# A fused attention and edge-filter kernel: engine orders written by hand, and steps and loads placed anew

## The chip, the cores and the metric

The kernel runs on one core of a Trainium2 chip. The metric is the device time of one execution in microseconds, and the median of several runs is compared. One execution of the kernel before was also taken by the hardware profiler. In what follows PE is TensorE, PEld its weight loads, DVE VectorE, ACT ScalarE, POOL GpSimd and SP the engine whose queue issues the DMAs.

## The reference

Two layers follow each other on `x` of shape (4, 512, 64, 64), all in float32.

```python
# layer 0: linear attention with an extra convolved head set
q, k, v = h @ wq.T, h @ wk.T, h @ wv.T                  # 512 -> 512 each, per pixel
qkv = concat([q, k, v]);  dw = depthwise_5x5(qkv);  pw = grouped_1x1(dw, groups of 8)
f = concat([qkv, pw]).reshape(B, 128 heads, 3 * 8, N)
query, key, value = relu(f[:, :, :8]), relu(f[:, :, 8:16]), f[:, :, 16:]
scores = einsum('bhdn,bhen->bhde', [value; 1], key)
out = einsum('bhde,bhen->bhdn', scores, query);  out = out[:8] / (out[8] + eps)
y = conv1x1(out, proj) * inv + shift + x                # folded batch norm, residual
# layer 1: edge maps, branches, attention, fuse
sobel, lap, diag, grad = fixed 3x3 depthwise filters of y, with abs, squares and square roots
ef = gelu(batch_norm(1x1 branch of each map))           # 4 branches, 512 -> 128 each
att = sigmoid(w2 @ gelu(w1 @ mean(ef)))                 # per image
z = w_fuse @ (ef * att);  out = gelu(layer_norm(z)) + y
```

## The kernel before, in words

The work is split by image `b` (4), and in each image by group `g` of 128 channels (`NG` = 4), so there are 16 groups. An image's 4096 pixels are cut into 8 strips of 512 (`NJ`), each strip made of every fourth row of one half of the image.

**A group** runs two lists of steps. `keys_and_values` projects the keys and the values of the 8 strips (`project`, `values`), transposes the keys (`turn`) and sums scores (`scores`). Between these steps it places what is left over from the group before: correlations of the second half of the image, both query convolutions, and divisions. `queries` projects the queries, convolves the keys (`convolve(KEY, 0)` and `convolve(KEY, 1)`), transposes the result (`conv_turn`), correlates it with the values (`correlate`) and divides. `convolve` issues 160 small 32x32 matmuls, each seen twice in the trace, so 320 matmul records and 320 weight loads for each of the 64 convolutions. The two convolutions of keys are called K0 and K1 here, those of queries Q0 and Q1.

**Value patches.** `values` writes the values to a scratch in DRAM (`near<-vt`), and `load_near` reads patches of it back (`near<-near`, 1056 KB each, 8 for each group). Three are loaded at the end of `keys_and_values`; each second `correlate` step frees a buffer and loads the next. In `queries` the first, second, third and fourth such load come after `co(0, 0)`, `co(0, 2)`, `co(1, 0)` and `co(1, 2)`; the last three of these stand directly ahead of K1, with no projection among them.

**Behind the groups** of image b + 1 runs what remains of image b, as three generators: `project_out` (Y: 32 steps, `yps` matmuls, `y` stored to DRAM), `edge_branches` (E: for 16 windows and 2 channel pairs the edge maps on DVE and ACT, then `br` matmuls) and `fuse_out` (F: `zps` matmuls, layer norm, output). Each generator yields a share of time, and `advance` runs its next step when the foreground's steps have used up as much (`pace`). The last image has no groups behind which it could run: its Y, E and F, and the F of image 2, are the tail. In the tail half of Y runs alone, then one step of the rest (second half of Y, then F of image 2) follows each yield of E, then F of image 3 runs alone.

**Order.** `tc.manual_schedule(engines={PE})` (L98) keeps the PE's instructions in the order in which the code issues them. The instructions of DVE, ACT and POOL, and the DMAs of the SP queue, are put in order by the scheduler, from its own costs. Each engine then runs its list strictly from the front, and a DMA whose data is not ready holds up those behind it. `ps` tiles in PSUM have 4 buffers, and the `quad` tiles 4.

Of the kernel before, what the change touches and what calls it, by code (L numbers as in the profile page):

```python
# [65 lines left out]

WAIT_Y, WAIT_E, WAIT_F = 20.0, 12.0, 16.0
# [13 lines left out]
def conv_seq_kernel(  # L81
# [16 lines left out]
    ctx.enter_context(tc.manual_schedule(engines={mybir.EngineType.PE}))  # L98
# [72 lines left out]

    def load_constants():
        nc.sync.dma_start(out=consts_sb, in_=consts)
        nc.sync.dma_start(out=vec_sb, in_=vec)
        nc.sync.dma_start(out=batt1_sb, in_=batt1)

        nc.scalar.activation(inv0, vec_sb[:, V_BNV, :], AF.Sqrt, bias=bn0_eps)
        nc.vector.reciprocal(inv0, inv0)
# [3 lines left out]

        gamma_row = work_tile("gamma_row")
        nc.sync.dma_start(out=inv0_row, in_=bn0[1])
        nc.sync.dma_start(out=gamma_row, in_=bn0[0])
        nc.scalar.activation(inv0_row, inv0_row, AF.Sqrt, bias=bn0_eps)
# [25 lines left out]

    xs = {}

    class Group:
# [15 lines left out]
        def load_mat(self, t):  # L231

            dp = gw.tile([P, 4, 48], F32, name="dp_sb", tag="dp_sb", bufs=2)
            nc.sync.dma_start(out=dp, in_=dpk[self.g, t // QUERY])
            self.mat[t] = gw.tile([P, 4, 40, 8], F32, name="mat", tag="mat")
            nc.gpsimd.tensor_tensor(  # L236
                self.mat[t],
                dp[:, :, 0:40].unsqueeze(3).to_broadcast([P, 4, 40, 8]),
                dp[:, :, 40:48].unsqueeze(2).to_broadcast([P, 4, 40, 8]),
                ALU.mult,  # L240
            )

        def load_x(self, j):
            xs[self.b, j] = []
            for n in range(2):
                xt = xst.tile([P, 2, 512], F32, name="xt")
                nc.sync.dma_start(out=xt, in_=x[self.b, j, :, 2 * n : 2 * n + 2, :])
                xs[self.b, j] += [xt[:, 0, :], xt[:, 1, :]]

        def project(self, t, j):  # L250
            half, k = STRIPS[j]
            if (self.b, j) not in xs:
                self.load_x(j)
# [5 lines left out]
            if t == QUERY and not (j in KV_ORDER[:2] and self.g < NG - 1):  # L259
                del xs[self.b, j]  # L260
# [4 lines left out]
            for n in range(4):  # L265
                nc.sync.dma_start(out=inps[t][r::4, n, b : b + 8, :], in_=rows(s)[32 * n : 32 * n + 32, :, :])
# [6 lines left out]
        def values(self, j):  # L273
# [8 lines left out]
            if j not in Q_ORDER[:2]:  # L282
                del xs[self.b, j]
# [5 lines left out]
            for a in range(2):  # L289
                for jp in range(2):  # L290
                    nc.sync.dma_start(
                        out=self.near_dram[jp, b + a : b + a + 7 : 2, 2 : W + 2, (k + 2) % 4, :].rearrange(
                            "c x d -> x c d"
                        ),
                        in_=vt[64 * a : 64 * a + 64, :, 2 * jp : 2 * jp + 2, :].rearrange("p c q d -> p c (q d)"),
# [37 lines left out]
        def fold_turn(self):  # L333
# [4 lines left out]
            nc.scalar.copy(self.st, t_ps[:, 0:P])  # L338
            self.p = work_tile("p")
            nc.sync.dma_start(out=self.p, in_=proj[self.g])  # L340

        def fold(self):
# [4 lines left out]
            nc.sync.dma_start(out=self.folded[0, :, self.g, :], in_=f)  # L347
# [24 lines left out]
        def divide(self, half):  # L372
            banks = self.spread_out(self.rec)
            for k in range(4):
# [3 lines left out]
                nc.sync.dma_start(out=self.heads[j, :, self.g, :], in_=q)  # L378
# [90 lines left out]
        def mix(self):  # L469

            self.pc = work_tile("pc")
            if self.b:
                nc.sync.dma_start(out=self.pc, in_=mixed[self.g])
                return
            rest = work_tile("projc")
            nc.sync.dma_start(out=rest, in_=projc[self.g])
            pw = mini.tile([P, 8], F32, name="pw")
            nc.sync.dma_start(out=pw, in_=pwk[self.g])
            pwb = mini.tile([P, 16, 8], F32, name="pwb", bufs=1)
            nc.vector.tensor_mul(  # L480
                pwb, bdmask.rearrange("p (h d) -> p h d", d=8), pw.unsqueeze(1).to_broadcast([P, 16, 8])
            )
            ps = ps_tile("mix")
            nc.tensor.matmul(ps, lhsT=pwb.rearrange("p h d -> p (h d)"), rhs=rest, start=True, stop=True)
            nc.scalar.copy(self.pc, ps)
            nc.sync.dma_start(out=mixed[self.g], in_=self.pc)
# [32 lines left out]
        def conv_fold(self):  # L519
# [5 lines left out]
            nc.sync.dma_start(out=self.folded[1, :, self.g, :], in_=f)  # L525
# [9 lines left out]
        def conv_divide(self, half):  # L535
            banks = self.spread_out(self.crec)
            for i in range(4):
                q = work_tile("cq")
                nc.vector.tensor_mul(q, self.conv[QUERY][i], banks[i])
                nc.sync.dma_start(out=self.cheads[half, self.g, i], in_=q)  # L540
# [3 lines left out]
        def keys_and_values(self, before):  # L544
# [12 lines left out]
            def q(method, *args):  # L557
                t = {"convolve": T_CONV, "correlate": T_CORR}.get(method, T_SMALL)
                return [(t, lambda: getattr(before, method)(*args))] if before else []

            def co(jp, first):
                return q("correlate", 1, jp, first) + q("correlate", 1, jp, first + 1)

            return sum([
                pj(KEY, 0), q("conv_sums"), pj(VALUE, 0), q("divide", 0), pj(KEY, 1), pj(VALUE, 1), co(0, 0), tr(0),
                pj(KEY, 2), co(0, 2), pj(VALUE, 2), sc(0), tr(1), co(1, 0), pj(KEY, 3), co(1, 2), pj(VALUE, 3), sc(1), tr(2),
                q("convolve", QUERY, 0), pj(KEY, 4), q("mix"), q("conv_weights"), sc(2), tr(3), pj(VALUE, 4),
                q("conv_heads"), q("conv_denominators", 0), pj(KEY, 5), q("conv_fold"), q("conv_divide", 0), sc(3), tr(4),
                pj(VALUE, 5), q("convolve", QUERY, 1), pj(KEY, 6), sc(4), tr(5), q("conv_denominators", 1), pj(VALUE, 6),
                [(0.0, self.load_wtab)], pj(KEY, 7), q("conv_divide", 1), sc(5), tr(6), pj(VALUE, 7),  # L570
                [(0.0, lambda: self.load_near(VALS))],
            ], [])

        def queries(self):
# [14 lines left out]
            def own(method, *args):  # L589
                return [(T_SMALL, lambda: getattr(self, method)(*args))]  # L590

            return sum([
                pj(0), own("scores", KV_ORDER[6]), own("turn", KV_ORDER[7]), pj(1), cv(0), pj(2), own("scores", KV_ORDER[7]), ct(0, 0), ct(0, 1), pj(3),
# [434 lines left out]
```

## Time and profile before

| | us |
|---|---|
| median of 3 runs (5157.64 to 5178.55) | 5158.51 |
| the profiled execution | 5156.95 |
| its span, first to last instruction | 5155.2 |
| PE busy in the span | 4721.2 |
| DVE busy | 2125.2 |
| ACT busy | 1622.7 |
| POOL busy | 384.0 |

The mean granted PE clock is 0.963 of full speed. The time of the profiled execution and its span differ by 1.75 us, which lie outside the first and last instruction. The groups fill the span up to about 4437 us; the tail is what follows.

### The profile page before, as it was taken

Reading aid. Unit: us, or ns where it says so; the run is one execution under the profiler, and the core shown is the slowest. Engines: PE = TensorE matmul, PEld = TensorE weight load, DVE = VectorE, ACT = ScalarE, POOL = GpSimd, SP = SyncE. Lnnn points to the kernel's source line nnn. Section 1 sums busy time; section 2 is a strip of 40 time slices with the busy share of each in tenths; the row PEclk is TensorE's granted clock in tenths of the full one; section 3 lists DMA queues with packets and bytes.
Section 4 is the critical chain, followed back from the end, with each engine's and each line's share of the span. In section 5 each row is a group of like instructions: output and inputs, shape, how many; then the busy total and the mean of one; then the engine's idle time right before and its main releaser. Section 6 shows DMA issues by size and latency. Waiting matters only on the chain. (4 is left out here: it accounts for less than half of the span.)

```text
span 5155.2 us, 107053 instructions
## 1 busy us (share of the span) xinstructions
PE 4721.2 (92%) x46362; PEld 2727.4 (53%) x46362; DVE 2125.2 (41%) x2960; ACT 1622.7 (31%) x2585; POOL 384.0 (7%) x291
## 2 busy tenths in 40 slices
PE   7899999998999999799999998989989998899877
PEld 4556555454566655344466655444446565345443
DVE  1222221113655625211456543431135556246975
ACT  1111111001444524200235442430024445125765
POOL 0000000000000003200000000320000000000225
PEclk9999999999999999899999999999999999899989
DMA  6777777775666666767667666567666665674535
GB/s 184 187 193 195 185 212 191 179 160 140 194 184 193 194 191 188 212 153 150 168 178 208 170 191 186 180 202 172 154 177 173 178 183 160 176 179 117 153 103 169
DMA packets 645992, 910.30 MB, mean 177 GB/s; under 512 B 323688, under 2 KB 394376, under 8 KB 627088
## 3 DMA queue, kind: packets, MB, share of 16 engines
q1 hardware_dynamic: 645520, 903.45, 65.5%
q8 instruction: 364, 5.96, 0.5%
q14 instruction: 108, 0.88, 0.1%
HBM read 622.13 MB, written 213.98 MB: 162 GB/s over the span
## 5 line engine op out<-in xcount | busy, mean ns | idle before, releaser
L256 PE MATMUL proj<-xt,w_sb 128*128 128x512 f32 x2048 | 959.6, 611 | 58.3 <-DMA xt<-in_x 47.2
L642 PE MATMUL yps<-hd,fold_sb 128*128 128x512 f32 x2048 | 904.3, 598 | 25.2 <-DMA hd<-heads 23.1
L390 PE MATMUL cv<-inp,mat 32*32 32x512 f32 x20480 | 771.7, 621 | 121.2 <-issue 112.0
L256 PEld LDWEIGHTS proj<-xt,w_sb 128*128 128x128 f32 x2048 | 382.8, 195 | 534.8 <-issue 457.1
L642 PEld LDWEIGHTS yps<-hd,fold_sb 128*128 128x128 f32 x2048 | 385.8, 191 | 510.5 <-issue 474.2
L390 PEld LDWEIGHTS cv<-inp,mat 32*32 32x32 f32 x20480 | 422.1, 105 | 433.5 <-issue 270.8
L717 PE MATMUL br<-maps,wbr_sb 128*128 128x256 f32 x2048 | 491.6, 393 | 56.6 <-ACT maps L700 33.7
L278 PEld LDWEIGHTS val<-w_sb,xt 128*128 128x128 f32 x4096 | 471.5, 192 | 31.6 <-issue 21.9
L717 PEld LDWEIGHTS br<-maps,wbr_sb 128*128 128x128 f32 x2048 | 395.6, 196 | 173.5 <-issue 55.8
L278 PE MATMUL val<-w_sb,xt 128*128 128x128 f32 x4096 | 484.1, 276 | 0.1
L795 PE MATMUL zps<-ef,wf_sb 128*128 128x512 f32 x1024 | 462.6, 604 | 21.0 <-DVE z L799 7.2
L262 ACT COPY strip<-proj 128x512 f32<-128x512 f32 x256 | 149.3, 583 | 1017.1 <-PE proj L256 952.8
L647 DVE SCALAR_TENSOR_TENSOR yt<-yps,shift,xr 128x512 f32<-128x512 f32 x128 | 96.1, 751 | 905.1 <-PE yps L642 833.7
L442 PE MATMUL corr<-near,ckt 128*32 128x160 f32 x8192 | 330.7, 313 | 28.1 <-DMA near<-near 23.0
L236 POOL TENSOR_TENSOR mat<-dp_sb 128x1280 f32<-128x1280 f32 x32 | 77.3, 2416 | 3484.1 <-PE cv L390 2959.3
L795 PEld LDWEIGHTS zps<-ef,wf_sb 128*128 128x128 f32 x1024 | 194.2, 193 | 263.8 <-issue 227.8
L442 PEld LDWEIGHTS corr<-near,ckt 128*32 128x32 f32 x8192 | 252.4, 110 | 130.0 <-issue 58.2
L690 DVE TENSOR_TENSOR maps<-dv 128x1054 f32<-128x1054 f32 x128 | 162.6, 1270 | 304.1 <-PE br L717 304.1
L724 ACT ACTIVATE ef_o<-br,shift,scale 128x256 f32<-128x256 f32 x256 | 142.4, 560 | 314.9 <-PE br L717 314.4
L306 ACT ACTIVATE kt<-tr 128x512 f32<-128x512 f32 x128 | 76.1, 595 | 496.5 <-PE tr L304 488.9
L354 DVE RECIPROCAL rec<-rec 128x512 f32<-128x512 f32 x64 | 214.5, 3351 | 1.4
L402 ACT ACTIVATE co<-cv 128x512 f32<-128x512 f32 x128 | 74.6, 597 | 438.5 <-PE cv L390 438.4
(124 smaller groups left out, 4096.6 us busy)
## 6 DMA issues: line engine op xcount, KB each, us to landing
xt<-in_x SPq DMA_DIRECT2D x400, 512.0 KB
near<-near SPq DMA_DIRECT2D x128, 1056.0 KB
inp<-strip SPq DMA_DIRECT2D x1024, 64.0 KB
win<-y SPq DMA_DIRECT2D x128, 396.0 KB
near<-vt SPq DMA_DIRECT2D x512, 66.0 KB
y<-yt SPq DMA_DIRECT2D x128, 264.0 KB
yr<-y SPq DMA_DIRECT2D x128, 264.0 KB
xr<-in_x SPq DMA_DIRECT2D x128, 256.0 KB
```

Of the source, the lines that this page charges most:

```text
L256: nc.tensor.matmul(ps, lhsT=self.w[t][:, c, :], rhs=xs[self.b, j][c], start=(c == 0), stop=(c == NCH - 1))
L262: nc.scalar.copy(s, ps)
L278: nc.tensor.matmul(ps[:, ts(c, P)], lhsT=xs[self.b, j][n][:, ts(c, P)], rhs=self.w[VALUE][:, n, :], start=(n == 0), stop=(n == NCH - 1),)
L354: nc.vector.reciprocal(rec, rec)
L390: nc.tensor.matmul(rows(banks[i])[32 * j : 32 * j + 32, :, c0:c1], lhsT=self.mat[t][q, j, (dx + 2) * 8 + 4 * b : (dx + 2) * 8 + 4 * b + 4, :],
L442: nc.tensor.matmul(self.banks[jj][32 * i : 32 * i + 32, 160 * b : 160 * b + 160], lhsT=self.held["c", i][:, at : at + 32], rhs=v[:, 4 * n ...
L642: nc.tensor.matmul(ps, lhsT=fold_sb[g // NG][:, g % NG, ts(c, P)], rhs=hd[g], start=(g == 0), stop=(g == 2 * NG - 1),)
L647: nc.vector.scalar_tensor_tensor(yt[:, :, 1 : W + 1], rows(ps), shift0[:, c : c + 1], rows(xr), ALU.add, ALU.add)
L690: nc.vector.tensor_sub(flat[:, half : 3 * half - 2], dvs[:, 2 : 2 * half], dvs[:, 0 : 2 * half - 2])
L717: nc.tensor.matmul(rows(ps)[:, 4 * n : 4 * n + 4, :], lhsT=wbr_sb[:, k, c, :], rhs=rows(maps[c // 2][:, slot[k], c % 2, :], WB)[:, :, 0:W] ...
L724: nc.scalar.activation(o[:, n, :], ps[:, 256 * n : 256 * n + 256], AF.Gelu, bias=shift1[:, k : k + 1], scale=scale1[:, k : k + 1], accum_o ...
L795: nc.tensor.matmul(ps, lhsT=wf_sb[:, k, ts(c, P)], rhs=ef[k], start=(k == 0), stop=(k == 3))
```

## The change

Five things are done.

1. ACT, DVE and POOL join the PE in `manual_schedule`: they run in the order of issue. The SP queue stays with the scheduler.
2. A clock of steps (`tick`) is added. `send` issues a store one step later than the code that computed its data, and `later` does the same for loads into buffers that a step frees, and for `make_mat`.
3. The lists of `keys_and_values` and `queries` are rearranged. In `queries`, `co(1, 0)` is followed by a projection, `co(1, 2)` by another, and K1 stands at the end, after `denominators(0)`; the `conv_turn`s of K1 move into the next group's list. `load_pc`, `load_p`, `load_w` and `load_wtab` become steps of their own, ahead of use. The halves of `x` are loaded in one fixed order (`x_order`) as buffers come free.
4. The generators are cut finer. A piece of E (one window, one channel pair) becomes `columns`, `gradient` and `roots` of the piece before, `across` and `laplacian`, with a yield after each, and its window is loaded one piece ahead. Y loads its folded weights in 8 parts of 256 KB beside `hd`, where it had 2 of 1024 KB. F spreads `norm` over the next strip's steps, as `variance`, a reciprocal and `finish`.
5. In the tail, 22 steps of F of image 2 are issued beside the first half of Y, and the second half of Y and 11 more steps of F are shared out over E by `FILL_Y`, `FILL_F` and `REST`.

```diff
-    ctx.enter_context(tc.manual_schedule(engines={mybir.EngineType.PE}))
+    ctx.enter_context(tc.manual_schedule(engines={engines.PE, engines.Activation, engines.DVE, engines.Pool}))
+    def later(issue, steps=1):
+        waiting.append((clock[0] + steps, issue))
+    def send(out, in_, steps=1):
+        later(lambda: nc.sync.dma_start(out=out, in_=in_), steps)
...
         # keys_and_values, foreground and left-over steps
-                q("convolve", QUERY, 0), pj(KEY, 4), q("mix"), q("conv_weights"), sc(2), tr(3), pj(VALUE, 4),
+                co(1, 2), ld("load_wtab"), ld("load_pc", of=before), pj(VALUE, 3), sc(1), tr(2), pj(KEY, 4),
+                q("convolve", QUERY, 0), pj(VALUE, 4), q("mix"), q("conv_weights"), sc(2), tr(3), q("conv_heads"),
...
         # queries
-                pj(0), own("scores", KV_ORDER[6]), own("turn", KV_ORDER[7]), pj(1), cv(0), pj(2), own("scores", KV_ORDER[7]), ct(0, 0), ct(0, 1), pj(3),
-                ct(0, 2), ct(0, 3), own("denominators", 1), own("fold_turn"), pj(4), own("divide", 1), pj(5), co(0, 0),
-                own("fold"), pj(6), co(0, 2), co(1, 0), co(1, 2), cv(1), pj(7), ct(1, 0), ct(1, 1), own("denominators", 0),
-                ct(1, 2), ct(1, 3),
+                pj(0), own("scores", KV_ORDER[6]), own("turn", KV_ORDER[7]), ld("load_mat", QUERY), pj(1),
+                ld("load_w", KEY, of=after), own("scores", KV_ORDER[7]), pj(2), cv(0), pj(3), ct(0, 0), ct(0, 1),
+                own("denominators", 1), ct(0, 2), ct(0, 3), ld("load_p"), own("fold_turn"), ld("load_w", VALUE, of=after),
+                pj(4), own("divide", 1), co(0, 0), pj(5), co(0, 2), own("fold"), co(1, 0), pj(6), co(1, 2), pj(7),
+                own("denominators", 0), cv(1),
...
         # project_out
+            for g in range(2 * NG):
+                nc.sync.dma_start(out=fold_sb[g // NG][:, g % NG, :], in_=folded[g // NG, :, g % NG, :])
+                load(0, g + 1)
+                yield WAIT_Y / (2 * NG)
...
         # edge_branches
+            for p in range(4 * NJ + 2):
+                ready = p // 2 - 1 if p >= 2 and p % 2 == 0 else None
+                if p < 4 * NJ:
+                    columns(p)
+                    load_window(p + 1)
+                    yield 3.0 * share
+                if 1 <= p <= 4 * NJ:
+                    gradient(p - 1)
+                if p < 4 * NJ:
+                    across(p)
+                if 1 <= p <= 4 * NJ:
+                    roots(p - 1)
+                    yield 4.5 * share
+                if ready is not None:
+                    branches(ready, (1, 2))
+                    yield 1.5 * share
+                if p < 4 * NJ:
+                    laplacian(p)
+                    yield 5.0 * share
...
     # start: the second strip's x is loaded ahead of the constants
+    load_x(2)
+    first.load_w(VALUE)
+    load_x(3)
     load_constants()
...
     # tail
-    for _ in range(1 + NCH * NJ // 2):
-        next(projected)
+    for n in range(6 + NCH * NJ // 2):
+        next(behind[0])
+        tick()
+        for _ in range(1 if n >= 6 else 2 if n >= 2 else 0):
+            next(projected)
+            tick()
```

## The prediction

> **What bounds the kernel now.** I read first the busy shares on the page, then whom the PE waited for, then the stretches around single convolutions and the tail.
>
> ```profile
> PE 4721.2 (92%) x46362; PEld 2727.4 (53%) x46362; DVE 2125.2 (41%) x2960; ACT 1622.7 (31%) x2585; POOL 384.0 (7%) x291
> ```
>
> The PE is the bound, so only its idle time and its slowed time can be won: 434 us are idle. Taking each kind of step at its undisturbed price (256 projections at 3.43 us, 128 Y steps at 6.87, 64 convolutions at 10.6, 128 `val` at 3.57, `br` at 3.45, `zps` at 3.43 and `corr` at 2.47, and some 370 us of small steps) the PE's work adds up to some 4460 us, so idle and slowed time make up about 690 us. The waits of the PE, longest sums first (us in total, times, longest):
>
> ```profile
> PE cv L390 <- issue: 112.0, 46, 4.4
> PE proj L256 <- DMA xt<-in_x: 47.2, 14, 12.1
> ...
> PE over L369 <- DVE rec L354: 23.6, 16, 4.6
> ...
> PE corr L442 <- DMA near<-near: 23.0, 7, 19.6
> PE heads_ps L511 <- ACT strip L262: 20.4, 1, 20.4
> PE mix L484 <- DMA projc<-in_projc: 14.2, 4, 4.9
> ```
>
> The largest is no wait for data at all: inside a convolution the PE runs out of instructions. Where that happens the stretches show: K0 of one group first, K1 of the same group below it (columns: stretch, its length, PE, PEld, DVE, ACT and POOL busy, granted clock, DMA share, GB/s).
>
> ```profile
> 679.10:689.70 10.60, 10.60 (x322) 6.56 (x321) 0.00 (x0) 1.09 (x3) 0.00 (x0) 1.00 0.70 225
> 725.00:744.40 19.40, 14.15 (x324) 7.08 (x320) 2.12 (x4) 0.00 (x0) 0.00 (x0) 0.91 1.01 279
> ```
>
> The same 320 matmuls take 10.6 us and 19.4 us. In K1 the DMA engines are full and the clock falls to 0.91. The timeline of another K1, SP's row above the PE's, shows what fills them:
>
> ```profile
> 347.56 5.12 SPq L427 DMA_DIRECT2D near<-near  x3
> ```
> ```profile
> 352.03 7.28 PE L390 MATMUL cv<-inp,mat 32*32 32x512 f32 x193
> 362.71 5.91 PE L390 MATMUL cv<-inp,mat 32*32 32x504 f32 x127 [3.40 <-issue]
> ```
>
> Three patch loads (3 x 1056 KB) start within 5 us of the convolution, and after 193 matmuls the PE stands for 3.40 us. Of the 46 such stalls in the timeline 24, with 70 of the 112 us, lie in K1. Fourteen K1s that stand free of other work last 19.2 us in the mean, 8.6 over the undisturbed 10.6; 16 of them lose 137 us. Q0 and Q1, with one or two patch loads near, lose about 2.2 us each (1.0 of stall, the rest slow clock).
>
> The tail is bound otherwise (same columns):
>
> ```profile
> 4600.00:4700.00 100.00, 100.00 (x279) 52.65 (x278) 50.61 (x76) 36.82 (x50) 0.00 (x0) 1.00 0.65 156
> 4700.00:4800.00 100.00, 85.24 (x264) 50.87 (x262) 91.92 (x117) 75.61 (x108) 20.07 (x14) 0.93 0.42 126
> 4800.00:4900.00 100.00, 79.04 (x226) 46.36 (x226) 98.77 (x115) 80.96 (x110) 30.23 (x22) 0.90 0.50 148
> ```
>
> While the second half of Y runs beside E the PE is full and DVE half idle; then F of image 2 joins E and DVE is full while the PE starves.
>
> **The change part by part.** The sum is made against the profiled execution, 5156.95 us (5155.2 of span and 1.75 outside), which stands 1.56 under the median of 5158.51.
>
> *Patch loads and K1.* In the new order the fifth, sixth and seventh loads of a group start after `co(0, 2)`, `co(1, 0)` and `co(1, 2)`, with `fold` (1.0 us) and a correlation (2.5), then a projection (3.4) and a correlation (2.5), then a projection and `denominators` (4.4) ahead of K1. So they start about 14, 10 and 4.4 us ahead, and earlier where a background step stands between. At the 279 GB/s above 3.17 MB need 11.4 us. Most has landed when K1 begins. I price the new K1 like today's Q0 and Q1: 8.6 - 2.2 = 6.4 us won, times 16, rounded to 100 us. Bounds: 0 if the queue keeps the loads at K1, 137 if nothing is left. The Trainium skill (Runtime: NRT & Kernel Launch, Instruction fetch mechanics) speaks against this part: blocks of 256 instructions are fetched by a DMA queue of their own while the block before runs, at a cost that is "mostly hidden". By that rule these 100 us would be 0. The trace differs: the piece between two stalls is often 128 matmul records, which with their weight loads are 256 instructions, and the stall comes with the loads. I take the trace.
>
> *Start.* The first stall, 12.14 us at 14 us into the run, is for the second strip's `xt`, which stands behind the constants and other writes in SP's queue. Now it goes ahead of them. After the stall 8 records took 6.70 us where 3.60 is usual:
>
> ```profile
> 26.53 6.70 PE L256 MATMUL proj<-xt,w_sb 128*128 128x512 f32 x8 [12.14 <-DMA xt<-in_x]
> ...
> 45.06 3.60 PE L256 MATMUL proj<-xt,w_sb 128*128 128x512 f32 x8
> ```
>
> That is 15 us; I take 12, since the first strip now shares the DMA engines with more.
>
> *The 20.4 us of `heads_ps`.* The release is named wrongly: the DVE's timeline shows a burst of 36 edge operations from 1218.8 to 1243.1 us ahead of the two small ones that the PE needs, after 15.1 us of waiting for `win`. In order of issue a step of E brings at most 5 DVE operations (`gradient` and `across`: 0.725 + 0.744 + 1.270 + 0.715 = 3.5 us). The burst goes; the wait for the first window remains possible: 15 us won.
>
> *The 19.6 us of `corr`.* SP's timeline has two `fold_sb` loads of 1 MB and eight `hd` loads ahead of the missing patch. They are now spread over eight yields. The skill speaks against it (DMA: Bandwidth & Descriptors, Bandwidth: batch to 1 MiB): its table has 138 GB/s at 64 KB and 341 at 1 MB, so 256 KB pieces at the worst would add 1.9 - 0.8 = 1.1 us each, 35 us of DMA time for 32 pieces. The trace has the DMA busy for 65.5% only, and the large load in front of the patch cost the PE 19.6. Taken: 18 won, with the cover that Y's first step comes after all eight.
>
> *Other waits.* Later `xt` waits (10.7 and 4.0): 10 won by the fixed order of halves. `over` after the reciprocal, `cv` after `weighed` (8.3), `corr` after `q` (3.5): 35 us now; the reciprocal of `denominators(0)` (3.35 us) gets K1 as cover, and `weigh` a projection: 18 won. `mix` and its loads (14.2): loaded some 7 us ahead, 12 won.
>
> *Tail.* A piece of E costs DVE 8.50 us (eleven rows, L683 to L709), 32 pieces 272. A strip of F costs DVE 4 x 0.746 + 3.35 + 4 x 0.989 = 10.3 and the PE 14.6. Today first half of Y to end of E takes 4447 to 4998: 551 us. New: 22 steps of F (about 4.5 strips) with 16 of Y are 66 + 110 = 176 us of PE. Then 14 pieces of E with 16 steps of Y: PE 14 x 3.45 + 110 = 158, DVE 131. Then 18 pieces with 3.5 strips of F: DVE 153 + 36 = 189, PE 113. Together 523: 28 won. In F of image 3 the PE's small waits (8.3 us from 5020 to 5131) shrink with 8 `z` buffers: 5 won.
>
> *What is added.* 24 more DMA issues on SP at 0.442 us are 11 us of a queue that has long waits of its own: 0, hidden by these. Eight small memsets on POOL (0.11 us): 0, POOL is 7% busy. `make_mat` (2.4 us on POOL) waits three steps and POOL's adds wait behind it; it is needed by the convolution some 15 us later. Stores go one step later: with 18 work tiles nothing waits at once. For new waits that order of issue brings on ACT and DVE the trace shows nothing; nearest is today's `br` after ACT `maps`, 33.7 us in 9 waits, mostly in the tail. Bounds: -10 (fewer changes of activation table) to +250 (below); I take 28, near that row.
>
> Sum: 100 + 12 + 15 + 18 + 10 + 18 + 12 + 28 + 5 - 28 = 190. 5156.95 - 190 = 4967, and on the median 4968.
>
> **The rivals.** *Slower: in-order ACT becomes the block.* In `laplacian` three ACT operations wait for four DVE operations (2.90 us), and behind them on ACT stand the copies that empty the PE's PSUM tiles. If in each of 128 pieces the PE waited for those 2.90 us, that is 371 us against 218 won: 5310. It decides from 218 / 128 = 1.7 us for each piece on. Against it: three free `ps` tiles hold some 10 us of PE work, DVE is only 54% busy while E runs in the groups (1105 of 2050 us in the three such stretches), and the abs-and-square block is 2.8 us. If half of it shows, 5124.
>
> *The loads stay at K1.* The scheduler still orders SP, and a load may be held up by a store that is not ready. Then 100 us are missing: 5067. The PE's waits for `near` would fall all the same.
>
> *Part is given back elsewhere.* A window or `hd` load comes late, or E in the tail is held by the exchange between DVE and ACT: 5067 to 5125.
>
> *Nothing changes:* gains and new waits cancel. It would be chance.
>
> **How the numbers follow.** The forecast (4870 to 5050) has 0.58, gains partly lost (5050 to 5125) 0.20, no change 0.06 (within 0.5%, 26 us, which is about what a measurement of this kernel can tell), slower 0.16. So faster 0.78. The low end is the sum with 137 for K1, a quarter more of the other 118 us and no new waits, 4870; the high end must reach to where only the slower case is left out, 5185. Beyond it lie 0.15, below 0.05.
>
> **What would show it.** Right: K1 at 12 to 14 us, `cv` after issue at 50 to 70 us in total, no PE wait over 10 us at the first `win` or at the start of Y, PE idle near 260 us, mean clock about 0.975, DVE over 90% for less than 250 us of the tail. Wrong: `proj` or `br` waiting for ACT `strip`, `maps` or `lap` with more than 100 us in total; K1 still at 19 us.

## The result, and the profile after

The kernel became slower. The median of 5 runs is 5214.93 us (5197.10 to 5231.97), against 5157.64 us for the kernel before (5153.78 to 5178.55): a ratio of 1.0104, with a 95% interval of 1.0070 to 1.0138. The forecast was 4968 us. The profiled execution took 5231.97 us, of which 5230.2 are its span; the mean granted clock is 0.957, where it was 0.963. It is the longest of the five, 17 us over their median, and sums from its trace carry that.

The page's row of busy times, in the kernel after:

```profile
PE 4743.6 (91%) x46362; PEld 2726.7 (52%) x46362; DVE 2135.3 (41%) x2960; ACT 1582.8 (30%) x2567; POOL 358.6 (7%) x299
```

The PE has the same 46362 matmul records. It is busy 22 us longer and idle for 486.6 us (span less busy), where 434 were idle before and 260 were forecast. Whom it waited for, in the kernel after (us in total, times, longest; `ksum_ps`, `heads_ps` and `hid_ps` are small matmuls of sums: of the keys, of the heads and of the pooled maps):

```profile
PE cv L429 <- issue: 92.0, 49, 4.8
PE br L804 <- DVE dv L758: 44.3, 6, 10.2
PE br L804 <- ACT maps L788: 42.0, 10, 6.5
PE proj L295 <- DMA xt<-in_x: 32.9, 9, 14.7
PE ksum_ps L536 <- DVE ktotal L534: 26.5, 8, 6.0
PE corr L481 <- DVE q L416: 25.6, 13, 10.2
...
PE hid_ps L880 <- DVE pooled L874: 24.1, 3, 11.4
...
PE heads_ps L554 <- DVE s_sb L360: 18.9, 9, 3.5
```

The waits that the change aimed at have shrunk: `cv` after issue from 112.0 to 92.0, `xt` from 47.2 to 32.9, `near` from 23.0 to 6.7, and those for `projc` are gone. In their place stand waits for DVE, most of them new. Summed by the engine that ended them, all rows of this view give 70.8 us for DVE before and 174.3 after; the waits for DMAs fell from 120.2 to 72.5, those for ACT are 96.0 and 105.5. The engine that a row names is inferred; where two end at nearly the same time it can be the other.

Two stretches around convolutions, K0 above and K1 below, of the same group that the prediction shows (columns: stretch, its length, PE, PEld, DVE, ACT and POOL busy, granted clock, DMA share, GB/s):

```profile
672.00:684.50 12.50, 11.58 (x322) 6.38 (x321) 0.00 (x0) 1.09 (x2) 0.00 (x0) 1.00 0.53 175
721.30:737.80 16.50, 12.86 (x325) 6.53 (x321) 4.04 (x2) 1.11 (x4) 0.00 (x0) 0.90 0.92 259
```

K1 takes 16.5 us instead of 19.4. The loads are spread as planned; SP's queue ahead of another K1, which starts at 527.07, shows one about every six microseconds. The last three start 14.6, 8.7 and 2.4 us ahead of it, where the prediction had 14, 10 and 4.4:

```profile
506.73 0.57 SPq L466 DMA_DIRECT2D near<-near  x1
512.43 0.56 SPq L466 DMA_DIRECT2D near<-near  x1
518.41 0.56 SPq L466 DMA_DIRECT2D near<-near  x1
524.71 0.56 SPq L466 DMA_DIRECT2D near<-near  x1
```

The tail, with the same columns as above:

```profile
4700.00:4800.00 100.00, 93.28 (x263) 52.47 (x264) 63.53 (x90) 45.90 (x66) 0.00 (x0) 0.95 0.66 162
4800.00:4900.00 100.00, 75.28 (x221) 47.53 (x219) 77.84 (x105) 62.31 (x89) 6.37 (x5) 0.86 0.38 103
4900.00:5000.00 100.00, 60.60 (x181) 41.64 (x182) 84.19 (x110) 66.23 (x92) 12.60 (x11) 0.77 0.32 93
```

In the late part of E, DVE was at 92 to 99% in the two stretches before. Now it is at 78 to 84%, and the PE is less busy too (75 and 61%, before 85 and 79%): neither engine is full.

Where a small wait comes from can be read off DVE's timeline around the key totals of the last group (start, length, operation; in brackets the idle time ahead of it and what ended it):

```profile
4369.54 0.70 DVE L793 TENSOR_TENSOR maps<-maps 128x524 f32<-128x524 f32 x1 [5.03 <-ACT maps L787]
4370.28 0.71 DVE L794 SCALAR_TENSOR_TENSOR maps<-lap,maps 128x524 f32<-128x524 f32 x1
4370.90 1.25 DVE L767 TENSOR_TENSOR maps<-dv 128x1054 f32<-128x1054 f32 x1
...
4377.00 0.71 DVE L758 SCALAR_TENSOR_TENSOR dv<-win,dv 128x528 f32<-128x528 f32 x1
4377.63 0.16 DVE L534 TENSOR_TENSOR ktotal<-ksum 128x4 f32<-128x4 f32 x1
```

DVE stood 5.03 us at `gradient` for ACT's squares (L787). Then it worked through eleven operations of E, and only then through the 0.16 us that the PE needed. The PE's timeline at that place:

```profile
4377.93 0.56 PE L536 MATMUL ksum_ps<-ktotal,consts_sb 128*128 128x4 f32 x2 [5.95 <-DVE ktotal L534]
```

### The profile page after: what moved, and what is told of

Same layout as the page of the kernel before. It is cut to its first block, busy times and chain, and to the rows that moved or that the text cites. A ratio compares the mean times of both kernels' runs of the same rounds, so it can differ in the third digit from the quotient of the medians.

```text
span 5230.2 us, 107148 instructions
## 1 busy us (share of the span) xinstructions
PE 4743.6 (91%) x46362; PEld 2726.7 (52%) x46362; DVE 2135.3 (41%) x2960; ACT 1582.8 (30%) x2567; POOL 358.6 (7%) x299
## 4 chain that ended last, share of the span: by engine, by line
PE 68%; issue 5%; DVE 5%; DMA 4%; ACT 2%; POOL 1%; SPq 1%; POOLq 0%; ACTq 0%; DVEq 0%
PE yps L700 15%; PE proj L295 12%; PE cv L429 11%; PE br L804 7%; PE zps L906 7%; PE val L317 6%; PE corr L481 5%; PE over L408 1%; PE tr L341 1%; DMA hd<-cheads 1%; DMA hd<-heads 1%; DMA xt<-in_x 1%; POOL z L939 1%; PE s L352 1%; DMA yr<-y 1%
## 5 line engine op out<-in xcount | busy, mean ns | idle before, releaser
L295 PE MATMUL proj<-xt,w_sb 128*128 128x512 f32 x2048 | 969.9, 617 | 41.2 <-DMA xt<-in_x 32.9
L429 PE MATMUL cv<-inp,mat 32*32 32x512 f32 (+1 forms) x20480 | 743.2, 608 | 92.4 <-issue 92.0
L804 PE MATMUL br<-maps,wbr_sb 128*128 128x256 f32 x2048 | 515.6, 408 | 115.1 <-DVE dv L758 44.3
L429 PEld LDWEIGHTS cv<-inp,mat 32*32 32x32 f32 x20480 | 405.1, 104 | 411.0 <-issue 281.7
L804 PEld LDWEIGHTS br<-maps,wbr_sb 128*128 128x128 f32 x2048 | 412.9, 205 | 237.0 <-ACT maps L788 94.9
L324 DVE COPY vt<-val 128x512 f32<-128x512 f32 x128 | 87.6, 685 | 442.3 <-PE val L317 436.3
L912 DVE TENSOR_SCALAR z<-zps,fbias 128x512 f32<-128x512 f32 x128 | 94.8, 741 | 413.5 <-ACT sq L910 162.3
```

The lines of the kernel that those rows point to most:

```text
L295: nc.tensor.matmul(ps, lhsT=self.w[t][:, c, :], rhs=xs[self.b, j][c], start=(c == 0), stop=(c == NCH - 1))
L429: nc.tensor.matmul(rows(banks[i])[32 * j : 32 * j + 32, :, c0:c1], lhsT=self.mat[t][q, j, (dx + 2) * 8 + 4 * b : (dx + 2) * 8 + 4 * b + 4, :],
L804: nc.tensor.matmul(rows(ps)[:, 4 * n : 4 * n + 4, :], lhsT=wbr_sb[:, k, c, :], rhs=rows(maps[2 * u + c // 2][:, slot[k], c % 2, :], WB)[:, ...
L912: nc.vector.tensor_scalar(zs[j, c], ps, fbias[:, c : c + 1], None, ALU.add)
```

## Experiments

The runs were made in four sets, each with its own runs of the kernel before, and ratios are to those. The kernel after was timed in its own set only, and its ratio of 1.0104 is uncertain by 0.0034 (18 us): differences from it below that are not read as effects. The SP queue stays with the scheduler in every run, so a difference includes what its new order there does.

**Which part of the change costs the time.** First the fixed order was taken back, all else kept.

```diff
-    tc.manual_schedule(engines={PE, Activation, DVE, Pool})
+    tc.manual_schedule(engines={PE})
```

> The changed kernel with one line undone: only the PE in the order of issue, ACT, DVE and POOL again ordered by the scheduler. Theory 1, the order of issue is what costs (the PE waits for small DVE and ACT results that stand behind edge operations and behind waiting operations: ksum_ps, heads_ps, hid_ps, den, corr after q, br, together some 110 us more than before): 5100 to 5140 us, and ksum_ps and heads_ps waits near 0. Theory 2, the new places of steps and the new pieces of E and F in the tail are what costs: 5195 to 5230 us, with those waits about as in the changed kernel. The on-record forecast, to which order of issue was nearly neutral: within 28 us of the changed kernel.

Measured: 5073.23 us, ratio 0.9873 (0.9858 to 0.9888). The other four parts of the change are a gain of 1.3%; the fixed order takes 2.3%, some 119 us, away.

Next, one engine at a time was given back to the scheduler.

```diff
+    tc.manual_schedule(engines={PE, Activation, Pool})     # e_dve
+    tc.manual_schedule(engines={PE, DVE, Pool})            # f_act
```

> The changed kernel with VectorE left to the scheduler, ScalarE, GpSimd and TensorE in the order of issue. The whole of the fixed order was worth 116 us (1.0104 of the kernel before, against 0.9873 with TensorE alone fixed). Theory A, VectorE's order is the cost (small VectorE operations such as the key sums, the head sums and the reciprocals stand behind E's long ones, and the PE waits for them): nearly all comes back, ratio 0.988 to 0.993, and the PE's wait for the key totals falls from 26.5 us to near 0. Theory B, ScalarE's order is the cost (the strip copies that empty the PE's PSUM tiles stand behind E's maps): little comes back, ratio 1.005 to 1.012. Theory C, it is the chain between both engines that counts, half each: about 0.999.

> The changed kernel with ScalarE left to the scheduler, VectorE, GpSimd and TensorE in the order of issue. Theory A (VectorE's order is the cost): ratio to the kernel before 1.005 to 1.012, the wait for the key totals stays near 26 us. Theory B (ScalarE's order is the cost): 0.988 to 0.993, and the waits of br for the maps fall below 20 us. Theory C, half each: about 0.999. If e_dve and f_act both stay near 1.01, the cost needs both orders freed together.

Measured: `e_dve` 5063.45 us, 0.9858 (0.9840 to 0.9876); `f_act` 5198.16 us, 1.0127 (1.0112 to 1.0141). Giving DVE alone back returns the whole cost, 2.5% or some 127 us; giving ACT alone back returns none. In `e_dve` the order of ACT and POOL stays fixed and costs nothing that can be measured (`a_sched`, with neither fixed, has 0.9873). What is not separated is whether DVE's order would cost as much with POOL's free: no run has that. The PE's 26.5 us at the key totals are gone in `e_dve`. DVE's waits, two of them in the kernel before:

```profile
DVE ktotal L491 <- ACT co L402: 248.6, 16, 20.1
DVE vt L285 <- PE val L278: 236.9, 74, 18.5
```

In the kernel after:

```profile
DVE yt L705 <- PE yps L700: 843.8, 113, 26.3
DVE vt L324 <- PE val L317: 436.3, 98, 22.1
...
DVE maps L767 <- PE br L804: 128.7, 12, 19.4
...
DVE maps L793 <- ACT maps L787: 108.0, 17, 13.3
```

The same view of `e_dve`:

```profile
DVE yt L705 <- PE yps L700: 724.9, 105, 28.5
DVE maps L767 <- PE br L804: 259.1, 53, 24.7
DVE vt L324 <- PE val L317: 243.7, 76, 20.6
...
DVE maps L793 <- ACT maps L787: 169.5, 37, 16.8
...
DVE ktotal L534 <- ACT co L441: 134.2, 14, 14.6
```

The scheduler does not spare DVE its stops: at `maps` there are more of them. It chooses where they happen. In `e_dve` DVE stands ready for the key totals 14 times, 134.2 us in all, with E's operations behind them, as in the kernel before (248.6 us). In fixed order E stands ahead, and the PE waits instead. The key totals of the last group in `e_dve`, for comparison with the rows above:

```profile
4241.89 0.16 DVE L534 TENSOR_TENSOR ktotal<-ksum 128x4 f32<-128x4 f32 x1 [9.72 <-ACT co L441]
4246.50 1.26 DVE L767 TENSOR_TENSOR maps<-dv 128x1054 f32<-128x1054 f32 x1 [4.45 <-PE br L804]
```

**Where it costs.** `g_tail` keeps the fixed order through the groups and leaves the tail to the scheduler.

```diff
     front.close()
+    order.close()                                   # fixed order ends
+    ctx.enter_context(tc.manual_schedule(engines={PE}))
```

> The changed kernel with all four engines in the order of issue through the groups and only TensorE fixed in the tail. From the profiles with and without fixed order some 68 of the 116 us lie in the tail and 48 ahead of it. Theory A, the two are separate: 68 us less than the changed kernel, ratio to the kernel before about 0.997 (0.994 to 1.000), the tail 684 us long in place of 752, the stretch of late E with the PE idle for under 60 us in place of 101. Theory B, the tail is slow because the groups deliver its first data late: less than 20 us come back, 1.006 or more.

Measured: 5130.57 us, 0.9993 (0.9984 to 1.0002). So some 57 us of the cost lie in the tail, near the 68 expected, and the rest ahead of it. In `g_tail` all three engines are freed there, so the share of each in the tail is not shown. The stretch from the last `yps` to the last `br` is 197 us long in `g_tail` (4792 to 4989), 248 in the kernel after (4829 to 5077).

**The tail's new order of work.** `d_tail` takes back the sharing: the first half of Y runs alone, and all 33 steps of F are shared out over E.

```diff
-REST = 16 * FILL_Y + 11 * FILL_F
+REST = 16 * FILL_Y + 33 * FILL_F
...
-    for n in range(6 + NCH * NJ // 2):
-        next(behind[0])                             # F beside Y
+    for n in range(2 * NG + NCH * NJ // 2):
+        next(projected)
```

> The changed kernel with the tail's sharing undone: the first half of Y of image 3 runs alone, and all of F of image 2 is shared out over E (REST counts 33 steps of F), pieces of E unchanged. Theory 1, the late part of E is held by the exchange between DVE, ACT and PE and not by the sum of DVE's work, so more F there is free while the PE stands anyway: 5145 to 5165 us. Theory 2, DVE's sum of work bounds it (4.5 strips at 10.3 us more there, 77 us less ahead): 5180 to 5195. The on-record sum, by which the sharing wins 28 us: 5240.

Measured: 5258.52 us, 1.0233 (1.0217 to 1.0250), some 67 us slower than the kernel after. From the last `over` of the groups to the last `br` it takes 662 us, 599 in the kernel after. Both theories were wrong, which had it faster without the sharing. The sum on record had the sign right and the size wrong: in the fixed order the sharing is worth more than the 28 us that I gave it.

**Is it latency in late E?** `i_lag` issues `br` one piece later. It has a fourth `maps` buffer for this and, to make room, fewer `ef` and `z` buffers in the F of image 3, which runs after E.

```diff
-                ready = p // 2 - 1 if p >= 2 and p % 2 == 0 else None
+                ready = (p - lag) // 2 if p >= lag and (p - lag) % 2 == 0 else None    # lag = 3 in the tail
```

> The changed kernel, with the br matmuls of the last image's E issued one piece later than they are now (a fourth maps buffer; to make room F of image 3 has 5 ef and 7 z buffers, which can only slow the stretch after E). Theory 1, in the late tail the time goes into the exchange: br waits for the newest maps, VectorE waits for ScalarE's squares, each with its list in fixed order. With a piece of slack the PE's waits of br for maps fall by 40 us or more, VectorE in late E is above 90% busy, and 25 to 50 us come back: ratio to the kernel before 1.001 to 1.0055. Theory 2, VectorE's own stops (for z after the squares, for yt after yps) set the pace, and br only waits for what is late anyway: under 15 us, 1.0075 or more, VectorE still near 80% busy.

Measured: 5227.00 us, 1.0136 (1.0119 to 1.0153): no gain. The late part of E in the kernel after, in `i_lag` and in `e_dve`, from a view of each (columns as above):

```profile
4830.00:5078.00 248.00, 146.51 (x436) 102.40 (x434) 205.27 (x262) 169.09 (x235) 31.17 (x24) 0.77 0.31 92
```

```profile
4793.00:5043.00 250.00, 159.35 (x486) 106.55 (x484) 211.06 (x271) 169.61 (x240) 31.03 (x24) 0.80 0.33 96
```

```profile
4685.00:4895.00 210.00, 136.80 (x438) 95.20 (x438) 187.98 (x247) 162.90 (x230) 41.89 (x24) 0.84 0.36 107
```

In `i_lag` the PE's waits of `br` for DVE `dv` and ACT `maps` in this stretch fall from 100.8 to 69.2 us, but all of its waits there only to 90.6: others, of `br` for ACT `ef_o` and of `zps`, took their place. From the last `yps` to the last `br` it is 243 us, where it was 248. So a later `br` alone does not set the stretch free. DVE is still busy for 84% and not for over 90%, as theory 1 asked; in `e_dve` it is 90%. DVE's stops in this stretch add up to 33.0 us in the kernel after, to 13.8 in `e_dve` and to 2.6 in `g_tail`. One of them in the kernel after, from DVE's timeline:

```profile
4902.20 0.75 DVE L912 TENSOR_SCALAR z<-zps,fbias 128x512 f32<-128x512 f32 x1 [5.06 <-POOL z L939]
4902.87 1.14 DVE L776 SCALAR_TENSOR_TENSOR maps<-win,maps 128x524 f32<-128x524 f32 x1
```

and the PE's timeline just after it:

```profile
4908.24 8.29 PE L804 MATMUL br<-maps,wbr_sb 128*128 128x256 f32 x28 [10.24 <-DVE dv L758]
```

An operation of F waits 5.06 us for POOL to give a `z` buffer free; E's laplacian stands behind it though nothing keeps it, and the PE waits 10.24 us, until the laplacian and ACT's squares of it are done. The 28 matmuls then take 8.29 us where 6.04 is usual (28 times 3.45 / 16). The granted clock is 0.76 over these 8.29 us, from which 6.04 / 0.76 = 7.9 us would follow. The Trainium skill (TensorE: Matmul & The Clock Gate, Part 1: The HAM clock gate) has the PE fall to half clock after an idle window of some 3.4 us; with a wait of 10.24 us ahead and a clock of 0.76 behind it the row agrees.

**Can the cost be placed away by hand?** `h_small` moves the two small steps with the clearest waits.

```diff
-  q("conv_turn", 1, 3), q("conv_sums"), ...   q("conv_heads"), q("conv_denominators", 0), pj(KEY, 5), q("conv_fold"), q("conv_divide", 0), ...
+  q("conv_turn", 1, 3), q("conv_total"), ...  pj(KEY, 2), q("conv_sums"), ...
+  q("conv_denominators", 0), pj(KEY, 5), q("conv_heads"), q("conv_divide", 0), ...  q("conv_fold"), ...
```

> The changed kernel, still with all four engines in the order of issue, with the two small steps moved for which the PE waits most in the groups: the matmul of the key totals one projection and one value strip later than VectorE's addition for it, and the head sums one projection later. In the profile of the changed kernel these are 26.5 us (key totals) and 21.7 us (head sums) of PE idle time. Theory 1, the cost of VectorE's fixed order sits in such named small waits and can be placed away: both vanish and 35 to 48 us come back, ratio to the kernel before 1.001 to 1.004. Theory 2, VectorE simply runs behind, having stood idle ahead of a strip that the PE had not finished, and the wait moves to the next small step: under 15 us come back, ratio 1.0075 or more, with new waits for q, csb or rec.

Measured: 5192.95 us, 1.0067 (1.0051 to 1.0083). The point lies between the theories, and its interval overlaps that of the kernel after. The two waits fell from 45.4 to 7.3 us (`ksum_ps` and `heads_ps` after `s_sb`), but those for the reciprocal at `over` rose to 30.9 us, from 12.9 (6.5, and 6.4 at a place that was put down to `csb`). So about half of the wait moved on, which lies between the theories too. A little of it the edit made itself, since `conv_fold` no longer stands ahead of the division: 0.53 us in each group of image 0, behind which no E runs.

`c_wfmean` moves another stop of DVE, `wf_mean` behind its 1 MB load (61.3 us in 3 waits), by two steps.

```diff
-            nc.vector.tensor_reduce(wf_mean, wf_sb, AX.X, ALU.add)      # ahead of the pooled sums of F
+            nc.vector.tensor_reduce(wf_mean, wf_sb, AX.X, ALU.add)      # two steps later, ahead of the attention scaling
```

> The changed kernel with F's two wf_mean operations on DVE moved from ahead of the pooled sums to just ahead of the attention scaling, two steps later (the shares of those yields are 4, 8, 4 for 4, 4, 8). Theory 1: in the order of issue these operations stop DVE until the 1 MB wf_sb has landed (61 us in three places, 33 at the longest), and the PE's waits for hid_ps (37 us) and part of corr after q (15 us) come from it: 5170 to 5190 us. Rival: F's start waits for the last branches and pooled sums anyway: 5205 to 5220.

Measured: 5199.90 us, 1.0125 (1.0109 to 1.0141): no gain. `hid_ps` now waits 28.5 us for the small weights `watt_sb` in its place.

The last set asked how DVE falls behind. `m_grad` exchanges two steps of E; `n_vt` issues the copy of a value strip one step later (a count of 1 in `later` is the end of the same step, 2 the end of the next); `o_both` does both.

```diff
 # m_grad
-    gradient(p - 1);  across(p);  roots(p - 1)
+    across(p);  gradient(p - 1);  roots(p - 1)
 # n_vt
-    nc.vector.tensor_copy(vt, ps) and its stores
+    later(copy, 2)                                  # the same, for the first six strips
```

> The changed kernel in its fixed order, with one pair of steps of E exchanged: across of the new piece now stands ahead of gradient of the piece before. In the changed kernel VectorE stands at gradient for ScalarE's squares of the piece before, 108 us in 17 stops, and what the PE needs of VectorE is queued behind it. Exchanged, ScalarE has 2.0 us more at each stop. Theory 1, these stops at the head of VectorE's queue are what the fixed order costs: VectorE's wait at gradient falls by 25 to 35 us and 15 to 35 us come back, ratio to the kernel before 1.004 to 1.0075. Theory 2, VectorE's stops are idle time that matters to nobody, and it is only the length of E's bursts that delays the small steps: under 8 us, 1.009 or more.

> The changed kernel in its fixed order, with the copy of a value strip out of PSUM (vt) issued one step later for the first six strips of a group. In the changed kernel VectorE stands 436 us for the PE to end such a strip, 244 us where VectorE is ordered by the scheduler, although E's work could run there. Theory 1, that is where VectorE falls behind: the stops fall by 150 us or more, and 20 to 50 us come back, ratio 1.001 to 1.0065. Theory 2, VectorE has time enough after those stops (it is busy for 41% of the span): under 10 us, 1.0085 or more; a PSUM tile is held longer, which can cost 10 to 20 us in waits of the PE for vt.

> Both exchanges, of m_grad and n_vt, in one kernel. If the stops at the head of VectorE's queue are the cost, the gains add up: 35 to 85 us less than the changed kernel, ratio 0.994 to 1.004. If not, it is the sum of two changes that do nothing: 1.008 or more.

Measured: `m_grad` 5248.43 us, 1.0179 (1.0156 to 1.0203); `n_vt` 5171.52 us, 1.0022 (1.0008 to 1.0035); `o_both` 5207.55 us, 1.0088 (1.0063 to 1.0112).

`n_vt` gains some 42 us by moving one copy. Its DVE row, and two of the PE:

```profile
DVE vt L325 <- PE val L317: 245.2, 51, 23.3
```

```profile
PE ksum_ps L542 <- DVE ktotal L540: 10.6, 4, 6.0
...
PE heads_ps L560 <- DVE s_sb L366: 7.3, 7, 2.9
```

The stops fall from 436.3 us to what the scheduler has, 243.7. The PE's waits at the two small steps that `h_small` moved fall from 45.4 to 17.9 us, though this edit does not touch them: DVE had stood at a strip which the PE had not finished, while E's operations, ready, stood behind it, and so came late to the small steps. By the times this was about a third of the whole cost, with an uncertainty of some 20 us. The trace does not give all 42 to it: `cv` after issue is 70.2 us for 92.0, and nothing in the edit explains that.

`m_grad` fell outside both theories, 39 us slower. Its DVE rows:

```profile
DVE maps L767 <- PE br L804: 208.0, 21, 22.6
...
DVE maps L793 <- ACT maps L787: 39.2, 6, 8.9
```

The stop at `gradient` did fall, by 69 us. But `across` needs a `maps` buffer that only `br` frees; put ahead, it stops DVE there instead, 79 us more, and now `gradient` and through it `roots` and `br` stand behind. In `o_both` the gain of the one and the loss of the other about cancel (-42 + 39 = -3, measured -8), which leaves the second of its two expectations.

**The part that was to gain.** `b_k1` is the kernel before with K1's new place alone; `j_k1x` adds the fixed order of the loads of `x`.

```diff
 # b_k1, in queries
-                own("fold"), pj(6), co(0, 2), co(1, 0), co(1, 2), cv(1), pj(7), ct(1, 0), ct(1, 1), own("denominators", 0),
-                ct(1, 2), ct(1, 3),
+                own("fold"), co(0, 2), co(1, 0), pj(6), co(1, 2), pj(7), own("denominators", 0), cv(1),
 # j_k1x, besides
-            if (self.b, j) not in xs: self.load_x(j)
+            done_x(self.b, j)                       # loads the next two halves as a strip's buffers come free
```

> The kernel before with one part of the change alone: in the lists, K1 goes to the end of the queries, a projection stands between the last two patch loads and a projection and the denominators between the last load and K1, and the four transposes of K1 move into the next group's list. If the gain seen at K1 (about 5.5 us each) is net: 5065 to 5085 us. If most of the instruction stalls only move to K0, Q0 and Q1 (in the changed kernel all convolutions together lost 57 us less, not 88): 5095 to 5110. If the moved steps cost as much elsewhere: 5150 to 5165.

> The kernel before with the changed kernel's places of K1 and of the turns after it (as in b_k1, 1.0038), and now also its one fixed order of the loads of x, issued as buffers come free in place of at the first use. In b_k1 the convolutions took 111 us less, but the wait for x rose from 47 to 113 us. Theory 1, the gain of K1 was given back because x is asked for only at its use, behind patch loads: the wait for x falls below 40 us and the kernel gains 70 us or more on b_k1, ratio 0.988 to 0.992. Theory 2, the queue moves the stall on to whatever is loaded last: the waits for the patches and for x together stay above 120 us and the ratio at 1.000 or more.

Measured: `b_k1` 5153.37 us, 1.0038 (1.0027 to 1.0049); `j_k1x` 5092.11 us, 0.9923 (0.9910 to 0.9936), some 59 us better, a little less than the 70 of theory 1. The PE's waits in `b_k1`:

```profile
PE proj L256 <- DMA xt<-in_x: 112.9, 15, 15.6
PE cv L390 <- issue: 62.9, 33, 4.4
```

and in `j_k1x`:

```profile
PE cv L400 <- issue: 82.6, 48, 5.7
PE ctr L425 <- ACT co L412: 51.5, 8, 17.2
PE corr L452 <- DMA near<-near: 42.8, 9, 25.0
...
PE proj L266 <- DMA xt<-in_x: 9.9, 2, 5.6
```

In `b_k1` the convolutions take 111 us less than before (busy and idle, 893 to 782), and the wait for `x` rises by 66: it is asked for at its use, behind the patch loads. Asked for early, it is nearly gone, and of the 103 us some 37 go on to `ctr`, `near` and the stall in `cv` (41.2, 35.5 and 62.9 us in `b_k1`). Some 11 of the 59 us are the start, since five halves of `x` go ahead of the constants here too: the fourth projection begins at 31.11 us, in `b_k1` at 42.38.

**Candidates.** `k_best` (from `a_sched`) and `l_best` (from `e_dve`) move K1's turns, the key totals and the second denominators by one projection and put F's small weights ahead of its large one.

```diff
-                pj(KEY, 0), q("conv_turn", 1, 0), q("conv_turn", 1, 1), ..., pj(VALUE, 0), ...
+                pj(KEY, 0), ..., pj(VALUE, 0), q("conv_turn", 1, 0), q("conv_turn", 1, 1), ...
```

> A candidate: the changed kernel with TensorE alone in fixed order (a_sched, 0.9873), K1's turns and the key totals one projection later, the denominators of Q1 one projection later, and F's small attention weights loaded ahead of its 1 MB one. In a_sched the PE waits 38.1 us for co at the turns, 19.4 us at the denominators and 28.4 us for the attention weights. If these are plain latencies: 50 to 80 us less than a_sched, ratio 0.973 to 0.978. If ScalarE's order, chosen by the scheduler, is what is late (co stands behind other work whatever the place): under 20 us, 0.984 or more.

> The same moves as k_best with VectorE alone left to the scheduler (e_dve, 0.9858). There the wait for co at the turns is already gone, and 12.6 us at the denominators and 28.7 us for the attention weights are left. If these are plain latencies: 25 to 40 us less than e_dve, ratio 0.978 to 0.981, and no better than k_best. If fixed ScalarE order and moved steps add up: below 0.975. If the small loads ahead only make the 1 MB load late: 0.985.

Measured: `k_best` 5086.21 us, 0.9864 (0.9845 to 0.9883); `l_best` 5070.13 us, 0.9830 (0.9810 to 0.9849). `k_best` is no better than `a_sched`: its waits for `co` fell only from 57.5 to 42.0 us, and the stall in `cv` rose from 75.6 to 90.2. `l_best` has the lowest ratio of all, 1.7% under the kernel before; against `e_dve` the intervals overlap.

## Why the prediction was wrong

*Two terms of the sum failed, and neither alone would have made the kernel slower.* The first is the last term, the 28 us for "new waits that order of issue brings on". It was measured at some 119 us (`a_sched`) to 127 (`e_dve`). The bounds of -10 to +250 held it; the choice of 28, near today's `br` after ACT `maps`, did not. That row shows what one wait costs. What a fixed order costs is decided by what stands behind each waiting instruction, on every engine that is fixed, and for DVE I had only looked at one place. There the prediction let at most five operations stand ahead of a small one, those of one step of E; the timeline above shows eleven, because DVE had stopped and several steps had gathered. With 119 for 28 the sum still gives 5156.95 - 218 + 119 = 5058 us.

*The second is the 85 us for single waits in the groups* (12 + 15 + 18 + 10 + 18 + 12). Without the order's cost the sum said 218 us won, and `e_dve` shows 1.4%, some 73. Its trace and that of the kernel before tell where the rest is missing, roughly: it spans 5044.5 us, 17 less than the run's median, and in its set the kernel before was 21 us faster too. All convolutions take 791 us in it, 893 before: 102 won, where 100 were forecast. From the last `over` of the groups to the end it takes 696 us, before 724: 28 won of 33. But outside convolutions the PE waits in the groups for 201.6 us, where it waited for 199.5, and 85 should have gone. The waits aimed at did shrink, `near` from 23.0 to 0.2 and the 20.4 of `heads_ps` and the 14.2 of `mix` to none. Others grew: `watt_sb` from 8.1 to 28.7, `hd` from 13.5 to 35.1, `corr` after `q` from 3.5 to 14.4, and `cden` and `proj` wait for DVE for 12.6 and 11.7, which they did not. Each wait was priced as if nothing would take its place. Why each new one came is not shown.

*The slower rival had the right mechanism on the wrong engine.* An in-order ACT was to be the block; `f_act` and `e_dve` show that ACT's order costs nothing that can be measured. The block is DVE, which E's operations, the strips and the PE's small steps share. The test given for "wrong", `proj` or `br` waiting for ACT with more than 100 us, was not met (`maps` 42.0 + 24.5), so it would not have caught this.

*Late E* was to take 189 us as 153 + 36 us of DVE work. The work was sized well (188 us of DVE in `e_dve`, 205 in the kernel after), the step "DVE without gaps" failed: 205 of 248 us. The first two stretches of the tail came near (192 and 158 us, forecast 176 and 158). In all the tail was to win 28 and, by `d_tail`, its sharing wins more, but the order loses 57 there.

*K1* was right in mechanism: the mean of the 16 K1s fell from 19.0 to 13.4 us, within the 12 to 14 asked for. In the trace of the kernel after only 57 of the 100 us arrived (all convolutions, busy and idle, 893 to 836), but these 836 are the most of all runs with K1's new place; the other fifteen have 782 to 831. In part the stall moved to a neighbour: in these sixteen traces it is 15 to 26 us in K1, 70 before, and 20 to 32 in Q1, 18 before. In K0 and Q0 it scatters (8 to 18, 8 before; 13 to 26, 15 before). All these stalls together were to be 50 to 70 us and are 63 to 92. If these stalls are fetches, which no run shows (in the trace before, the eleven pairs of stalls that share a convolution all stand 128 records apart), then the rule of "mostly hidden", which would have given 0, is too low here.

*The start* was right: the fourth projection begins at 30.70 us, where it began at 45.06, 14 us against 12 forecast. `near` (18 taken, 16 measured) and the loads of `mix` (12 taken, 14 measured, of which 4.1 came back as a stall of `mix` after issue) too, as single waits of the kernel after. `xt` as a whole, the stall at the start among it, fell by 14 of some 22 us; its longest wait is still 14.7. The burst ahead of `heads_ps` is gone as one wait of 20.4, and came back as eleven small ones of 21.7 in sum, which is the first failing term again.

## What to carry to other kernels

When an engine's order is fixed by hand, go through its queue instruction by instruction: for each one that can wait, name what stands behind it and who waits for that. Let a copy out of PSUM follow a step later than the matmul that feeds it (`n_vt`); but moving an operation past another only helps if it does not itself wait for something later (`m_grad`). It should help to put short operations for the bound engine ahead of long filler, as the scheduler does in `e_dve`; no run does that by hand. Fix the engines one at a time: here ACT and POOL could be fixed beside the PE at no cost, and DVE cost more than all other changes gained. And do not add up waits as if each were won by itself: where several stand close, another can take the place.

## What was not expected of the hardware

The stall of the PE inside a convolution does not belong to the patch loads alone. It is longer in Q1 in all sixteen traces with K1's new place (20 to 32 us, 18 before), and it appears where no patch load is near. The K0 at 672.00 has one of 0.92 us, with no patch load started in the 30 us ahead of it and the DMA engines at 0.53, while the K0 at 679.10 in the kernel before has none with them at 0.70. So neither the patch loads nor how busy the DMA engines are decides it alone. What sets it off was not tried. That K0s stall more than before is not shown: in the kernel after it is 13.6 us, 8.1 before, but `f_act`, with the same lists, has 7.7.
